# Gathering a block's last places for its first nodes alone, and a number of places of its own for each block

## The chip, the core and the metric

The kernel runs on one core of one Trainium2 chip. The metric is the device time of one execution, in microseconds. Before the change it is 5551.11 us, the median of three runs (5551.11 to 5564.75). One execution was recorded by the hardware profiler; its span, from the first to the last instruction, is 4044.6 us.

The core's engines run side by side, each through its own queue in order: TensorE (PE, with its weight loads PEld), VectorE (DVE), ScalarE (ACT), GpSimd (POOL) and SyncE (SP). Here SP issues plain DMAs, and POOL issues the indirect ones (row gathers by a list of indices).

## The reference

Sixteen graphs of 1024 nodes with 64 channels pass through four layers. Each layer normalizes the node features, and adds its result to them. The adjacency is sparse: each pair of nodes is joined with a chance of some 1.6%, and each node to itself. Layers 0, 1 and 3 are products with the weighted adjacency. Layer 2 is the one that matters here: a degree-dependent rule removes some neighbours, and each node then gets, channel by channel, a weighted sum of three quantiles over the neighbours that are left:

```python
sv = jnp.sort(jnp.where(valid[..., None], x[:, None, :, :], big), axis=2)
m = valid.sum(-1)
for tau, wt in zip((0.25, 0.5, 0.75), (0.25, 0.5, 0.25)):
    pos = jnp.clip(tau * (m - 1.0), 0.0)
    lo, hi, frac = floor(pos), ceil(pos), pos - floor(pos)
    agg += wt * (sv[lo] * (1 - frac) + sv[hi] * frac)
```

So for each node the features of its neighbours have to be brought together and sorted in part, for each of the 64 channels.

## The kernel before

Everything runs on one core, one graph after another, with up to four graphs in work at once. The function `direct_path` makes six streams, each a generator over the sixteen graphs:

- `adjacency` loads the adjacency by rows (SP), makes its transpose by PE and ACT, applies the removal rule, and stores for each node a row of 1024 keys (`keys_d`) that says which nodes are its neighbours. It also ranks the nodes by their number of neighbours, most first, and so makes `node`, the node at each rank, and `pos`, the rank of each node.
- `layers` computes layers 0 and 1 and the normalized input of layer 2, and stores the latter in memory (`h_d`, one row of 64 values per node, and a row 1024 of zeros).
- `neighbour_lists` takes the ranked nodes in eight blocks of 128, one node to a partition. For each block an indirect DMA loads the key rows (`k`, line 1019), and the DVE's MAX8 finds eight neighbours at a time (lines 1034 to 1050). The list becomes `index` (line 1056), where an unused place points to the row of zeros. The same stream makes the weights of the places (`far`, `wts`) and notes in `bad` whether a node has more neighbours than its block has places; if one has, another, general path computes everything anew after this one.
- `gathers` brings the rows: for each place of each block one indirect DMA on POOL writes 128 rows of 64 values, one to a partition, into `raw` (line 1165).
- `sorts` sorts, on the DVE, the places of `raw` against each other, with min and max between `raw` and a second buffer `other` (line 1208), and adds up the places that the quantiles need (line 1231). The pairs follow from the number of places (`cap`) of the group.
- `tail` gathers the results back into the order of the nodes (`res`, line 1251, eight indirect DMAs on POOL), and computes the rest of layer 2 and layer 3, with the transposed adjacency loaded again in tiles (`at`, by SP).

The blocks form five groups (line 38), each `(first block, blocks, places, fewest neighbours)`:

```python
GROUPS = [(0, 1, 38, 17), (1, 1, 20, 15), (2, 2, 18, 12), (4, 2, 16, 10), (6, 2, 13, 1)]
```

Blocks of a group share a `raw` tile and a sorting program. A graph has 38 + 20 + 2 x 18 + 2 x 16 + 2 x 13 = 152 row gathers. There is one `raw` buffer per group (`raws`, one buffer), so the gathers of group k of a graph can't be written before the sort of group k of the graph before has left it; they may run ahead of their own sort by about a graph.

The order of the instructions on each engine is written out when the program is built. A planner holds a clock per engine (`clk.dve`, `clk.pool`, ...), each stream says when it can go on, and the first stream in the list that is due gets the next turn. The planner counts 1.27 us for a row gather. What it fixes is the order alone: at run time each engine waits on semaphores for what its next instruction needs, and an instruction that waits holds up those behind it on its engine.

Of the kernel before, what the change touches and what calls it, by code (L numbers as in the profile page):

```python
# [7 lines left out]
F32 = mybir.dt.float32  # L8
F16 = mybir.dt.float16
BF = mybir.dt.bfloat16  # L10
I32 = mybir.dt.int32
# [6 lines left out]
P = 128  # L18
C = 64
# [19 lines left out]

E_ID, E_ONE, E_CAP, E_LOW, E_CN, E_Q, E_END = 0, 128, 256, 264, 272, 280, 320  # L40
J_ID, J_BIG, J_OFF, J_ST, J_ROW, J_ONE, J_PI, J_NI, J_END = 0, 128, 256, 384, 896, 1920, 2048, 2176, 2184
KB = 4


def _span(cap, low):

    return (low - 1) // 4, -(-3 * (cap - 1) // 4)
# [62 lines left out]
def _program(cap, low):  # L110


    home, out = [0] * cap, []
    for layer in _network(cap, low):
        for greater in (True, False):
            items = [(home[i], home[j], i, j) for i, j, a, b in layer if (a if greater else b)]
            out += [(greater, p) for p in _patterns(items)]
        for i, j, _, _ in layer:
            home[i] ^= 1
            home[j] ^= 1  # L120
    lo, hi = _span(cap, low)
    return out, _patterns([(home[q], 0, q, q - lo) for q in range(lo, hi + 1)])
# [587 lines left out]
def direct_path(ctx: ExitStack, tc: tile.TileContext, t: dict, out: bass.AP, flag):  # L710
# [3 lines left out]
    nc = tc.nc  # L714
# [3 lines left out]
    const = ctx.enter_context(tc.tile_pool(name="const", bufs=1))  # L718
    loads = ctx.enter_context(tc.tile_pool(name="loads", bufs=2))
    graph = ctx.enter_context(tc.tile_pool(name="graph", bufs=1))  # L720
    nodes = ctx.enter_context(tc.tile_pool(name="nodes", bufs=2))
# [4 lines left out]
    dram = ctx.enter_context(tc.tile_pool(name="dram", bufs=2, space=bass.MemoryType.DRAM))  # L726
# [57 lines left out]
    clk = Clock()  # L784

    def after(dve=0.0, pe=0.0, act=0.0, lat=0.3):

        clk.dve += dve
        at = clk.dve
        if pe:  # L790
            clk.pe = at = max(clk.pe, at) + pe
        if act:
            clk.act = at = max(clk.act, at) + act
        return at + lat
# [215 lines left out]
    def neighbour_lists(b):  # L1010


        g = state[b]
        ks = []

        def load_keys(i):
            if i < NB:
                k = lists.tile([P, N], F16, name="k", bufs=KB)
                nc.gpsimd.indirect_dma_start(k, None, g["keys_d"],  # L1019
                                             bass.IndirectOffsetOnAxis(ap=g["node"][:, i:i + 1], axis=0))  # L1020
                clk.pool = max(clk.pool, clk.dve) + 1.3
                ks.append((k, clk.pool + 3.5))

        for i in range(KB):
            load_keys(i)
        total = sum(n * -(-cap // 8) * 8 for _, n, cap, _ in GROUPS)
        found = lists.tile([P, total], F32, name="found", bufs=1)
        m = g["m"]
        o = 0
        for b0, n, cap, _ in GROUPS:  # L1030
            for i in range(b0, b0 + n):
                src, at = ks[i]
                yield at
                nc.vector.max(out=found[:, o:o + 8], in_=src)  # L1034
                clk.dve += 1.15
                yield clk.dve
                less, before = src.bitcast(I16), None
                for r in range(1, -(-cap // 8)):


                    least = found[:, o + 7:o + 8]
                    if r == 1:
                        ts(less, src, least, None, op0=ALU.subtract)  # L1043
                    else:
                        ts(less, less, before, least, op0=ALU.add, op1=ALU.subtract)  # L1045
                    before = least
                    most = nodes.tile([P, 8], U16, name="most")
                    nc.vector.max(out=most, in_=less.bitcast(U16))  # L1048
                    o += 8
                    ts(found[:, o:o + 8], most.bitcast(I16), 0.0, least, op0=ALU.min, op1=ALU.add)  # L1050
                    clk.dve += 1.8
                    yield clk.dve
                o += 8
                load_keys(i + KB)
        index = lists.tile([P, total], I32, name="index")
        ts(index, found, -1.0, float(N), op0=ALU.mult, op1=ALU.add)

        s = nodes.tile([P, 2, NB], F32, name="s")
        tt(s[:, 0], m, cap8, ALU.is_gt)
        tt(s[:, 1], m, low8, ALU.is_lt)  # L1060
        tt(s[:, 0], s[:, 0], s[:, 1], ALU.max)
        tt(bad, bad, s[:, 0], ALU.max)

        at = nodes.tile([P, 3, NB], F32, name="at")
        for k in range(3):
            ts(at[:, k], m, (k + 1) / 4, -(k + 1) / 4, op0=ALU.mult, op1=ALU.add)
        far = lists.tile([P, 3, QT], F32, name="far", bufs=1)
        o = 0
        for b0, n, cap, low in GROUPS:
            lo, hi = _span(cap, low)  # L1070
            k = hi + 1 - lo
            tt(far[:, :, o:o + k * n].rearrange("p t (q i) -> p t q i", i=n),
               cf[:, None, E_Q + lo:E_Q + hi + 1, None].to_broadcast([P, 3, k, n]),
               at[:, :, None, b0:b0 + n].to_broadcast([P, 3, k, n]), ALU.subtract)
            o += k * n
        act(far, far, AF.Abs)
        for k, w in enumerate((0.25, 0.5, 0.25)):
            act(far[:, k], far[:, k], AF.Relu, bias=wcol[:, k:k + 1], scale=-w)
        g.update(index=index)
        done.add(("index", b))  # L1080
        yield after(1.7, act=1.7)
        wts = lists.tile([P, QT], F32, name="wts", bufs=3)
        tt(wts, far[:, 0], far[:, 2], ALU.add)
        tt(wts, wts, far[:, 1], ALU.add)
        clk.dve += 0.4
        g.update(wts=wts)
        done.add(("lists", b))
# [65 lines left out]
    def gathers(b):  # L1153
        g = state[b]
        yield max(g["rows_at"], clk.pool)
        for k, (b0, n, cap, _) in enumerate(GROUPS):
            while not (b == 0 or ("sort", b - 1, k) in done):
                yield None
            raw = raws.tile([P, cap, n * C], F32, name=f"raw{k}")
            o = sum(c * -(-r // 8) * 8 for _, c, r, _ in GROUPS[:k])  # L1160
            clk.pool = max(clk.pool, clk.dve)
            for s in range(cap):
                for i in range(n):
                    at = o + i * -(-cap // 8) * 8 + s
                    nc.gpsimd.indirect_dma_start(raw[:, s, i * C:(i + 1) * C], None, h_ds[b % 3],  # L1165
                                                 bass.IndirectOffsetOnAxis(ap=g["index"][:, at:at + 1], axis=0))
                clk.pool += 1.27 * n
                if s % 4 == 3:
                    yield clk.pool - 3
            g[f"raw{k}"] = (raw, clk.pool + 4)  # L1170
            done.add(("gather", b, k))
        done.add(("gathers", b))
# [141 lines left out]
    wcol = const.tile([P, 3], F32, name="wcol")  # L1314
    for k, w in enumerate((0.25, 0.5, 0.25)):
        nc.vector.memset(wcol[:, k:k + 1], w)
    programs = [_program(cap, low) for _, _, cap, low in GROUPS]
    h_ds = [dram.tile([N + 1, C], F32, name=f"h_d{k}", bufs=1) for k in range(3)]
    for h_d in h_ds:
# [2 lines left out]
    def over_graphs(step, *needs):  # L1322
# [8 lines left out]
        over_graphs(layers, ("rows", 0), ("tail", 3)),  # L1331
        over_graphs(tail, ("sorts", 0)),
        over_graphs(gathers, ("index", 0), ("layers", 0)),
        over_graphs(neighbour_lists, ("keys", 0), ("gathers", 2), ("sorts", 3)),
        over_graphs(sorts, ("lists", 0)),
    ]
# [40 lines left out]
def _constants():  # L1377

    import numpy as np

    p = np.arange(P)
    ef = np.zeros((P, E_END), np.float32)
    ef[p, E_ID + p] = 1
    ef[:, E_ONE:E_ONE + P] = 1
    for b0, n, cap, low in GROUPS:
        ef[:, E_CAP + b0:E_CAP + b0 + n] = cap
        ef[:, E_LOW + b0:E_LOW + b0 + n] = low
    ef[:, E_CN:E_CN + NB] = 512 * N + N - 1 - (p[:, None] + P * np.arange(NB))
    ef[:, E_Q:E_END] = np.arange(E_END - E_Q)
    eh = np.zeros((P, J_END), np.float32)  # L1390
    eh[p, J_ID + p] = 1
    eh[p, J_BIG + p] = 2048
    eh[:, J_OFF:J_OFF + P] = 1
    eh[p, J_OFF + p] = 0
    eh[:, J_ST:J_ST + N // 2] = p[:, None] < np.arange(N // 2)
    eh[p, J_ST + p] = 2050
    eh[0, J_ROW:J_ROW + N] = -1024 - np.arange(N)
    eh[0, J_ONE:J_ONE + P] = 1
    eh[:, J_PI:J_PI + P] = p
    eh[:, J_NI:J_NI + NB] = p[:, None] + P * np.arange(NB)  # L1400
    return {**_general_constants(), "ef": ef, "eh": eh.astype(np.float16)}
# [73 lines left out]
```

## Time and profile before

| | |
|---|---|
| time, median of three runs | 5551.11 us |
| span of the profiled execution | 4044.6 us |
| DVE busy | 3476.7 us, 86% |
| POOL busy | 2951.5 us, 73% |
| PE busy | 2039.3 us, 50% |
| ACT busy | 1411.8 us, 35% |
| row gathers | 2432, 1096 ns each in the mean |
| key loads, result gathers on POOL | 128 and 128 |
| DMA | 372.57 MB, 92 GB/s in the mean |

Busy time is what an engine spent in recorded instructions. The gap between two instructions counts as idle time, and each group's row says what ended it: `<-issue` means that nothing was waited for that the profile shows, a name means that this instruction or DMA was awaited. A line of the waits reads: who waited, for what, how many us in total, how often, and the longest. The times in a timeline run from the start of the span. On POOL, the recorded length of an indirect DMA is POOL's own part of it.

### The profile page before, as it was taken

To read this page: it belongs to the slowest core of one execution; us is meant where nothing else is said; L and a number is where in the kernel's file an instruction comes from. 1 tells how busy PE (TensorE), PEld (TensorE's weight loads), DVE (VectorE), ACT (ScalarE), POOL (GpSimd) and SP (SyncE) were. 2 spreads that over 40 slices of the span, in tenths; PEclk is the share of its full clock that TensorE was granted. 3 is DMA by queue.
4 is the path that set the end of the run, shared out by engine and by line. 5 is a ranking of instruction groups with operands and counts; after the bars stand their busy time and mean duration, and the time that the engine had idled before them with its cause. 6 is when DMAs were issued, how large, how long until landed. Compare 5 with 4: busy or idle time off the path is not lost.

```text
span 4044.6 us, 34028 instructions
## 1 busy us (share of the span) xinstructions
PE 2039.3 (50%) x8387; PEld 980.5 (24%) x8387; DVE 3476.7 (86%) x9450; ACT 1411.8 (35%) x2594; POOL 2951.5 (73%) x2707
## 2 busy tenths in 40 slices
PE   7565574264735546473554647455454745540303
PEld 3223231121313122231322213132221313110101
DVE  2649998997999999998998989899998999997583
ACT  6544442342425333342533434253432424320000
POOL 0277777777777777777777777777777777777771
PEclk8676676576767767776675767677677776765656
DMA  2343543444434454543444444443535444442312
GB/s 88 115 87 88 120 111 53 110 92 90 117 55 126 86 120 94 109 104 50 125 90 115 94 96 114 53 138 74 130 83 105 108 62 112 76 109 37 68 26 53
DMA packets 251857, 372.57 MB, mean 92 GB/s; under 512 B 120160, under 2 KB 120352, under 8 KB 251648
## 3 DMA queue, kind: packets, MB, share of 16 engines
q0 software_dynamic: 92640, 117.88, 23.5%
q1 hardware_dynamic: 158864, 251.87, 18.4%
q8 instruction: 68, 1.11, 0.1%
q14 instruction: 141, 1.16, 0.1%
q10 hardware_dynamic: 144, 0.56, 0.0%
HBM read 256.84 MB, written 113.25 MB: 92 GB/s over the span
## 4 chain that ended last, share of the span: by engine, by line
POOL 41%; DVE 33%; issue 13%; PE 5%; DMA 5%; ACT 2%; DVEq 0%; POOLq 0%; ACTq 0%
POOL raw L1165 37%; DVE other L1208 8%; DVE raw L1208 7%; DVE most L1048 5%; PE pt L845 4%; POOL res L1251 3%; DMA raw<-h_d,index 2%; DVE found L1034 2%; DVE agg L1231 2%; DVE k L1045 1%; DMA k<-keys_d,node 1%; DVE found L1050 1%; DVE k L1043 1%; ACT adjt L1125 1%; DVE nb L874 1%
## 5 line engine op out<-in xcount | busy, mean ns | idle before, releaser
L1165 POOL DMA_INDIRECT raw<-h_d,index x2432 | 2666.0, 1096 | 757.5 <-issue 724.7
L1208 DVE TENSOR_TENSOR other<-raw 128x128 f32<-128x128 f32 (+7 forms) x1488 | 766.5, 533 | 73.4 <-DMA raw<-h_d,index 60.3
L1208 DVE TENSOR_TENSOR raw<-other 128x256 f32<-128x256 f32 (+10 forms) x1424 | 679.1, 490 | 4.3
L845 PE MATMUL pt<-adjt,ha 128*65 128x512 f32 (+1 forms) x1024 | 492.9, 644 | 299.3 <-DVE ha L1115 299.2
L881 PE MATMUL pt<-ef,a 128*128 128x128 f32 x1024 | 232.7, 391 | 389.4 <-ACT adjt L882 354.5
L1295 PE MATMUL tm<-at,ha 128*64 128x512 f32 x512 | 286.0, 677 | 54.9 <-DMA at<-adjt_d 52.4
L845 PEld LDWEIGHTS pt<-adjt,ha 128*65 128x65 f32 (+1 forms) x1024 | 150.0, 150 | 621.9 <-issue 569.6
L1048 DVE MAX8 most<-k 128x8 uint16<-128x1024 uint16 x224 | 275.0, 1228 | 7.7
L881 PEld LDWEIGHTS pt<-ef,a 128*128 128x128 f32 x1024 | 173.5, 203 | 441.8 <-ACT adjt L882 391.0
L922 PE MATMUL pt<-eh,nbt 128*128 128x512 f16 (+3 forms) x1024 | 210.0, 364 | 125.9 <-ACT nbt L911 125.4
L1019 POOL DMA_INDIRECT k<-keys_d,node x128 | 131.0, 1023 | 191.2 <-DVE node L1004 122.0
L956 ACT ACTIVATE nb<-pt 128x1024 f16<-128x1024 f32 x128 | 130.8, 1022 | 390.2 <-PE pt L952 248.3
L834 PE MATMUL pt<-ef,res 128*64 128x128 f32 x128 | 30.2, 418 | 425.7 <-DVE res L1255 335.3
L1034 DVE MAX8 found<-k 128x8 f32<-128x1024 f16 x128 | 156.3, 1221 | 99.2 <-DMA k<-keys_d,node 99.2
L887 ACT ACTIVATE nb<-nb 128x512 f16<-128x512 f16 x256 | 159.6, 628 | 206.2 <-DVE nb L876 119.4
L978 ACT ACTIVATE sink<-pt,neg 128x1024 f16<-128x1024 f32 x128 | 140.4, 1121 | 244.9 <-PE pt L973 244.9
L1208 DVE TENSOR_TENSOR other<-raw,other 128x256 f32<-128x256 f32 (+4 forms) x592 | 206.9, 354 | 5.4
L846 ACT COPY big<-pt 64x1024 f32<-64x1024 f32 (+1 forms) x32 | 32.2, 1007 | 505.9 <-PE pt L845 505.9
L1251 POOL DMA_INDIRECT res<-agg_d,pos x128 | 146.1, 1141 | 83.5 <-DMA agg_d<-agg 43.0
L927 ACT ACTIVATE ab<-pt,sf 128x512 f16<-128x512 f32 x256 | 161.8, 687 | 124.6 <-DVE gone L932 67.8
L1208 DVE TENSOR_TENSOR raw<-raw,other 128x256 f32<-128x256 f32 (+3 forms) x608 | 203.0, 338 | 0.0
L1208 DVE TENSOR_TENSOR raw<-other,raw 128x128 f32<-128x128 f32 (+5 forms) x560 | 196.1, 357 | 3.1
(154 smaller groups left out, 4068.0 us busy)
## 6 DMA issues: line engine op xcount, KB each, us to landing
a<-in_adj_dram SPq DMA_DIRECT2D x128, 512.0 KB, 3.6
adjt_d<-adjt SPq DMA_DIRECT2D x128, 512.0 KB, 5.7
at<-adjt_d SPq DMA_DIRECT2D x256, 256.0 KB, 3.8
raw<-h_d,index POOLq DMA_INDIRECT x2432
keys_d<-nb SPq DMA_DIRECT2D x128, 256.0 KB, 2.3
x<-in_x_dram SPq DMA_DIRECT2D x16, 256.0 KB, 2.9
h_d<-h SPq DMA_DIRECT2D x16, 256.0 KB, 4.2
agg_d<-agg SPq DMA_DIRECT2D x16, 256.0 KB, 2.8
```

The lines of the kernel that those rows point to most:

```text
L845: nc.tensor.matmul(p[p0:p0 + n, s], h[:, j, :n], adjt[:, j, s], start=j == 0, stop=j == NB - 1)
L881: nc.tensor.transpose(p[:, u * P:(u + 1) * P], a[:, j * P:(j + 1) * P], identf)
L887: act(nb[:, i, s], nb[:, i, s], AF.Copy, accum_out=mn[:, q, i:i + 1])
L922: nc.tensor.matmul(p[:, o:e], nbt[:, j, :], stair[:, :e - o], start=j % 4 == 0, stop=j % 4 == 3)
L927: act(ab[:, s], p[:, s], AF.Abs, bias=sf[:, 2 + q, i:i + 1], scale=2.0)
L978: act(sink, p, AF.Sign, bias=neg[:, i:i + 1], accum_out=over[:, i:i + 1])
L1034: nc.vector.max(out=found[:, o:o + 8], in_=src)
L1048: nc.vector.max(out=most, in_=less.bitcast(U16))
L1165: nc.gpsimd.indirect_dma_start(raw[:, s, i * C:(i + 1) * C], None, h_ds[b % 3], bass.IndirectOffsetOnAxis(ap=g["index"][:, at:at + 1], axi ...
L1208: tt(to, v0, v1, ALU.max if greater else ALU.min)
L1251: nc.gpsimd.indirect_dma_start(res[:, i, :], None, g["agg_d"], bass.IndirectOffsetOnAxis(ap=g["pos"][:, i:i + 1], axis=0))
L1295: nc.tensor.matmul(p[:C, :], ha[:, j, :C], ats[k], start=j == 0, stop=j == NB - 1)
```

## The change

Within a block the nodes stand in order of their number of neighbours, so a high place is used by the first few nodes alone. In block 0, with its 38 places, the first nodes decide the number. The change gives each block its own number of places, and brings the last 16 places of block 0 in another way:

- Blocks get 22, 20, 18, 17, 16, 14, 13 and 12 places. The places between this number and the group's `cap` are filled with zeros by ACT (`zcol`), as a gather of row 1024 would have done.
- For block 0, places 22 and 23 are brought for its first 64 nodes, 24 to 27 for the first 32, and 28 to 37 for the first 12: 2 x 64 = 128, 4 x 32 = 128 and 10 x 12 = 120 rows. Each of these sets is one indirect DMA, with one pair of node and place to a partition, into `packed`.
- For that, SP stores the three corners of `index` to memory (`pack_d`) and loads them back with one index to a partition (`pack`). And SP stores the packed rows to memory (`rows_d`, in the program after the ninth place is issued) and loads them into their places in `raw` (after the seventeenth).
- The table of places against which `bad` is judged (`E_CAP`) says the new numbers, node by node for block 0.

Row gathers of a graph go from 152 to 132, and 3 packed ones are added. The sorting programs and `GROUPS` stay as they are. The diff, without the table's part:

```diff
+PLACES = [22, 20, 18, 17, 16, 14, 13, 12]
+PACKS = [(22, 2, 64), (24, 4, 32), (28, 10, 12)]
...
         ts(index, found, -1.0, float(N), op0=ALU.mult, op1=ALU.add)
+        pack_d = dram.tile([len(PACKS), P], I32, name="pack_d")
+        pack = nodes.tile([P, len(PACKS)], I32, name="pack")
+        for l, (s0, ns, nn) in enumerate(PACKS):
+            nc.sync.dma_start(pack_d[l, :ns * nn].rearrange("(n s) -> n s", s=ns), index[:nn, s0:s0 + ns])
+        for l, (s0, ns, nn) in enumerate(PACKS):
+            nc.sync.dma_start(pack[:ns * nn, l:l + 1], pack_d[l, :ns * nn].rearrange("(n o) -> n o", o=1))
...
             clk.pool = max(clk.pool, clk.dve)
+            for i in range(n):
+                if PLACES[b0 + i] < cap:
+                    z = raw[:, PLACES[b0 + i]:cap, i * C:(i + 1) * C]
+                    nc.scalar.copy(z, zcol[:, :, None].to_broadcast([P, cap - PLACES[b0 + i], C]))
+                    clk.act = max(clk.act, clk.dve) + 0.2 + (cap - PLACES[b0 + i]) * C / 1400
+            if k == 0:
+                packed = nodes.tile([P, len(PACKS) * C], F32, name="packed", bufs=1)
+                for l, (s0, ns, nn) in enumerate(PACKS):
+                    nc.gpsimd.indirect_dma_start(packed[:ns * nn, l * C:(l + 1) * C], None, h_ds[b % 3],
+                                                 bass.IndirectOffsetOnAxis(ap=g["pack"][:ns * nn, l:l + 1], axis=0))
+                    clk.pool += 1.27
+                rows_d = dram.tile([len(PACKS), P, C], F32, name="rows_d")
             for s in range(cap):
+                if k == 0 and s == 9:
+                    for l, (s0, ns, nn) in enumerate(PACKS):
+                        nc.sync.dma_start(rows_d[l, :ns * nn], packed[:ns * nn, l * C:(l + 1) * C])
+                if k == 0 and s == 17:
+                    for l, (s0, ns, nn) in enumerate(PACKS):
+                        nc.sync.dma_start(raw[:nn, s0:s0 + ns, :],
+                                          rows_d[l, :ns * nn].rearrange("(n s) c -> n s c", s=ns))
                 for i in range(n):
+                    if s >= PLACES[b0 + i]:
+                        continue
+                    clk.pool += 1.27
                     at = o + i * -(-cap // 8) * 8 + s
                     nc.gpsimd.indirect_dma_start(raw[:, s, i * C:(i + 1) * C], None, h_ds[b % 3],
                                                  bass.IndirectOffsetOnAxis(ap=g["index"][:, at:at + 1], axis=0))
-                clk.pool += 1.27 * n
                 if s % 4 == 3:
                     yield clk.pool - 3
```

More of the change, by code (lines that the diff above doesn't have):

```diff
@@ L1078, in neighbour_lists @@
             act(far[:, k], far[:, k], AF.Relu, bias=wcol[:, k:k + 1], scale=-w)
-        g.update(index=index)
+        g.update(index=index, pack=pack)
         done.add(("index", b))
@@ L1316, in direct_path @@
         nc.vector.memset(wcol[:, k:k + 1], w)
+    zcol = const.tile([P, 1], F32, name="zcol")
+    nc.vector.memset(zcol, 0.0)
     programs = [_program(cap, low) for _, _, cap, low in GROUPS]
@@ L1385, in _constants @@
     for b0, n, cap, low in GROUPS:
-        ef[:, E_CAP + b0:E_CAP + b0 + n] = cap
+        ef[:, E_CAP + b0:E_CAP + b0 + n] = PLACES[b0:b0 + n]
         ef[:, E_LOW + b0:E_LOW + b0 + n] = low
+    for s0, ns, nn in PACKS:
+        ef[:nn, E_CAP] = s0 + ns
     ef[:, E_CN:E_CN + NB] = 512 * N + N - 1 - (p[:, None] + P * np.arange(NB))
```

## The prediction, made before the changed kernel ran

> **What bounds the kernel now.** I read the page's busy line first, then GpSimd's groups and timeline, then the DVE's waits by stretch.
>
> ```profile
> PE 2039.3 (50%) x8387; PEld 980.5 (24%) x8387; DVE 3476.7 (86%) x9450; ACT 1411.8 (35%) x2594; POOL 2951.5 (73%) x2707
> ...
> POOL 41%; DVE 33%; issue 13%; PE 5%; DMA 5%; ACT 2%; DVEq 0%; POOLq 0%; ACTq 0%
> ...
> L1165 POOL DMA_INDIRECT raw<-h_d,index x2432 | 2666.0, 1096 | 757.5 <-issue 724.7
> ```
>
> By busy share the DVE looks like the bound and POOL (GpSimd) looks slack. But the chain gives POOL more than the DVE, and almost all the idle time before POOL's gathers is "issue": nothing was waited for. The timeline shows what that is:
>
> ```profile
> 1999.92 0.95 POOL L1165 DMA_INDIRECT raw<-h_d,index  x1 [0.30 <-issue]
> 2001.18 1.01 POOL L1165 DMA_INDIRECT raw<-h_d,index  x1 [0.30 <-issue]
> 2002.49 0.97 POOL L1165 DMA_INDIRECT raw<-h_d,index  x1 [0.30 <-issue]
> ```
> ```profile
> 188.00:3955.00 3767.00, 2925.32 (x2672) 0.70 0.43 92
> ```
>
> Each gather pays 0.30 us between instructions. The last line is POOL from its first row gather to its last: 2672 instructions in 3767 us, 1.410 us each. Of the 842 us "idle" in it, 2672 x 0.30 = 802 is that gap. POOL is full from 188 to 3955. A graph has 152 row gathers, 8 key loads and 8 result gathers: 168 x 1.410 = 236.9 us. The DVE needs 3476.7 / 16 = 217.3. So POOL sets the period, and the DVE is close behind. Where the DVE waits, by stretch (columns: total us, times, longest; then busy and counts of PE, PEld, DVE, ACT, POOL):
>
> ```profile
> 0.00:240.00 240.00, 159.53 (x746) 81.02 (x746) 88.15 (x194) 132.52 (x247) 57.74 (x68) 0.79 0.34 92
> 240.00:3640.00 3400.00, 1801.99 (x7414) 863.50 (x7413) 3139.81 (x8519) 1265.91 (x2324) 2641.05 (x2406) 0.71 0.44 98
> 3640.00:4045.00 405.00, 77.75 (x229) 35.94 (x228) 248.76 (x739) 13.38 (x23) 252.75 (x235) 0.57 0.27 46
> ```
> ```profile
> DVE found L1034 <- DMA k<-keys_d,node: 96.0, 12, 15.9
> DVE wts L1083 <- ACT far L1078: 41.7, 9, 12.7
> DVE den L1131 <- PE pt L1120: 26.5, 13, 3.6
> DVE other L1208 <- DMA raw<-h_d,index: 10.0, 2, 9.5
> ...
> DVE res L1255 <- DMA res<-agg_d,pos: 6.0, 1, 6.0
> ```
> ```profile
> DVE other L1208 <- DMA raw<-h_d,index: 50.3, 6, 13.7
> DVE res L1255 <- DMA res<-agg_d,pos: 47.0, 2, 32.0
> ```
>
> The DVE is idle 152, 260 and 156 us in the three stretches, 568 together. The first list is the middle: 112 of its 260 end with something POOL issued (key loads 96, rows 10, results 6). The second is the end: 97 of 156.
>
> **The Trainium skill.** "DMA: Bandwidth & Descriptors", section "Anatomy of one DMA — SWDGE (gpsimd) path", gives a fixed cost of about 2.0 us per DMA, most of it the receipt of the write. This trace agrees for the queues on SP: 2.3 us to landing for keys_d, 4.2 for h_d. "Perfetto Trace Analysis", section "DMA Instruction — SWDGE (GPSIMD)", says that the recorded end is when the descriptors are written, not when data has moved. The trace fits: the gathers follow each other at 1.3 us without waiting for their own landings, so a removed gather saves POOL its whole pitch. "SBUF — State Buffer", section "SBUF: two separate sides", says a DVE instruction in a two-port mode keeps GpSimd from writing descriptors; the spread here (0.94 at least, 1.096 mean) would fit, but this trace does not show the cause, and I keep the mean.
>
> **The change, part by part.**
>
> *Removed gathers.* Places per block go from 38, 20, 18, 18, 16, 16, 13, 13 (152) to 22, 20, 18, 17, 16, 14, 13, 12 (132), and 3 packed gathers are added: 135, 17 fewer. 17 x 1.410 = 24.0 us of POOL per graph, 384 us in all. POOL's period becomes 151 x 1.410 = 212.9 us, under the DVE's 217.3. The bound changes hands, so the kernel can't gain the 384. What it can gain is the DVE's idle time that POOL causes.
>
> *The DVE's work.* The sorting programs still take caps of 38, 20, 18, 16, 13, so no DVE instruction of weight is removed or added: 3477 us stay.
>
> *Zero fills on ACT.* Four copies a graph: 1024 columns for block 0, then 64, 128 and 64. Nearest rows: 128x1024 copies take 1.01 to 1.05 us, tiny ones 0.17 to 0.30. About 1.8 us a graph, 29 in all, on an engine that is 35% busy. Each waits until the sort of the graph before has left the buffer. Behind it in ACT's queue stand copies that free PSUM for PE and the keys' activations; but the planner puts the fill where the DVE has already been told to finish that sort, so I take 0 to 2 us a graph and use 0.
>
> *Index packing on SP.* Three stores and three loads of a few hundred bytes, two landings in a row: 2 x 2.0 (the skill's price) to 2 x 4.2 (h_d), 4 to 8.4 us. For the last graph the index is written at 3575.5 us, while its gathers must start near 3953 - 160 x 1.41 = 3727: hidden by 150 us. Only in the first graph (index 188.2, first gather 188.7) is it bare: I take 6 us.
>
> *Rows through memory.* Three stores that wait for the packed gathers, three loads that wait for those stores. SP issues in order, so while it waits, the loads of the next adjacency rows, the stores of keys and the third layer's tiles queue behind it; PE and then the DVE would feel it. The packed gathers are issued ahead of nine others (nine x 1.41 = 12.7 us), and the loads come eight places (11 us) after the stores, against landings of 2 to 4.2 us. If POOL is where the planner thinks, SP waits for nothing. The planner counts 1.27 us for a gather that takes 1.41, so POOL may be late: 0 to 15 us a graph. Since POOL now has slack every graph in which to catch up, I take 1 us.
>
> *The sum*, by the DVE's idle time. Start: 13 fewer gathers before the first sort (38 to 25) give 13 x 1.25 = 16, less 6 for packing and the rest not waited for: -8. Middle: 112 at most; POOL still issues key loads among row gathers, so I leave a quarter of the 96 and charge 1 us a graph for SP: -112 + 24 + 14 = -74. The end: POOL's last 135 + 8 gathers take 143 x 1.41 = 202 us, less than the DVE's 249 busy us there, so the 50 us for rows go; of the results' 47 the last graph's 32 are mostly a chain with nothing beside it, 15 go: -65. Idle time 568 - 147 = 421, span 3477 + 421 = 3898 us, 147 less (3.6%).
>
> *From the span to the time.* The measured time is 5551.11 and the traced span 4044.6. No view shows the other 1506.5 us. If they lie outside the span, 147 us pass through unchanged: 5404. If untraced executions are longer throughout, the gain grows by 5551.11 / 4044.6 = 1.372 to 202: 5349. I take the middle, 5376, and keep both.
>
> **The rivals.**
>
> *More: untraced executions are longer because the gathers are.* 1506.5 us over 2703 POOL DMAs would be 0.56 each, 1.97 instead of 1.41. Then POOL stays far from the DVE, and the saving is 272 x 1.97 = 536: 5015. For it: POOL is the full engine. Against: nothing shows a gather of that length as usual.
>
> *Nothing to speak of.* The DVE's waits are replaced by others of its own (wts on ACT and den on PE are there already, 68 us in the middle), and only the end gains: 0 to 65 us, 5486 to 5551. For it: 86% busy leaves little. Against: 209 us of its idle time end with POOL's DMAs.
>
> *Slower: SP becomes the bound.* If each graph waits on SP for both chains (two pairs of landings, 8 to 16 us) and for a late POOL (15), less what overlaps, some 20 us x 16 = 320 are added against 147 saved: +173, 5724. For it: SP serves five streams in order, and both chains are new waits in it. Against: the slots left for the landings (12.7 and 11 us) exceed them, and a POOL with 4 us of slack a graph does not fall behind for long.
>
> **How the numbers follow.** Forecast 0.62, more 0.10, nothing 0.13 (half of it within 0.3%, half a small gain), slower 0.15. So faster 0.62 + 0.10 + 0.065, about 0.79; same 0.06; slower 0.15. The likeliest gives 5376. The range: upward it takes in the small gains, no change, and a first bit of the slower rival: 5570, with about one in eight above it. Downward, all 217 us (8 + 112 + 97) gone at 1.372 would be 298, so 5253; I go to 5215 for part of the "more" rival, with some 6 in 100 below.
>
> **What would show it.** In the new trace POOL's indirect DMAs should fall from 2688 to 2416, and its idle time should be ended in part by the DVE (sorts leaving their buffers), not only by issue. The DVE's share should rise from 86% to near 89%, the waits for k fall from 96 us to some 25, those for rows at the end from 50 to near none. ACT's fills should sum to about 29 us. Wrong would be: SP waiting for the packed gathers for more than a few us a graph, with new DVE waits on adjacency rows, on PE's third-layer sums or on keys; POOL still full; or a span that falls while the time does not.

## The result and the profile after

In the first comparison the changed kernel took 4721.66 us (median of 4 runs, 4694.21 to 4753.48) and the kernel before 5557.93 us (median of 4, 5551.11 to 5579.64): a ratio of 0.849, 95% interval 0.843 to 0.855. That is 836 us less, where 175 were forecast. The sign was right, the size was not, and the time lies below the range.

One plain fact is needed to read every number below. The kernel before took 5551 us only in that first comparison; in four later ones, which met other conditions, it took 4036 to 4040 us, and in one of them the changed kernel took 3933.35 us (median of 4, 3931.77 to 3937.70): a ratio of 0.976, interval 0.974 to 0.979. So there are two results to explain: 2.4% under the conditions that the profile of before shows, and 15% under the others. The later comparisons ran on four chips (numbers 0, 5, 4 and 9); the first one's is not on record, so it is open whether its conditions belong to one chip or to one time.

The page of the changed kernel from the first comparison, the lines that answer to those shown of before:

```profile
span 4717.7 us, 34351 instructions
...
PE 2141.2 (45%) x8387; PEld 1020.2 (22%) x8387; DVE 3494.2 (74%) x9451; ACT 1434.6 (30%) x2658; POOL 2620.3 (56%) x2435
...
DVE 48%; another core or an unknown queue 21%; issue 9%; PE 8%; POOL 6%; ACT 5%; DMA 3%; SPq 0%; DVEq 0%; ACTq 0%; POOLq 0%
...
L1197 POOL DMA_INDIRECT raw<-h_d,index x2112 | 2278.8, 1079 | 1236.9 <-issue 827.3
```

The span is 4717.7 us in an execution that took 4719.47: the time is all inside the span. The work is what was counted on: 2112 row gathers at 1079 ns, 48 packed ones, DVE at 3494 us as before. But the DVE is busy for 74%, not 89%, and POOL for 56%: nobody is full. And 21% of the chain's time goes to something that the profile cannot name.

The same kernel under the later conditions:

```profile
span 3929.9 us, 34351 instructions
...
PE 2016.5 (51%) x8387; PEld 961.6 (24%) x8387; DVE 3470.3 (88%) x9451; ACT 1434.4 (36%) x2658; POOL 2697.9 (69%) x2435
...
DVE 41%; POOL 14%; PE 7%; issue 5%; DMA 5%; ACT 2%; SPq 0%; DVEq 0%; ACTq 0%; POOLq 0%
...
L1197 POOL DMA_INDIRECT raw<-h_d,index x2112 | 2350.3, 1113 | 785.0 <-issue 754.6
```

Here the chain has gone over from POOL (41% before) to the DVE, and the DVE's share is 88%. The instructions are the same in both traces and last nearly as long (the DVE is busy 24 us more in the first, POOL 78 less; PE, at a mean clock of 0.657 against 0.706, 125 more, at 45% of the span). What makes up the 788 us is idle time: the DVE's is 1223.5 us against 459.6.

**Where the 788 us are.** Two lists of waits, first the changed kernel in the first comparison, then under the later conditions (columns: us in total, times, longest).

```profile
ACT big L850 <- remote: 447.3, 11, 77.8
...
ACT nb L960 <- remote: 328.9, 30, 34.1
...
PE pt L1130 <- ACT big L850: 209.9, 15, 32.7
DVE den L1141 <- PE pt L1130: 200.1, 14, 32.5
```
```profile
ACT big L850 <- PE pt L849: 464.3, 32, 18.3
...
DVE den L1141 <- PE pt L1130: 36.2, 15, 12.2
```

"remote" means that the wait ended with a semaphore update (the signal that work is done) near which no work was recorded to end. ACT's copy of the messages (L850) normally starts when PE's sums for them (L849) are done, and waits 18.3 us at most. In the first comparison it stood up to 77.8 us and pulled PE, then the DVE, behind it. One such place in the timeline of that comparison (start, duration, instruction, idle time before it):

```profile
2333.11 16.89 PE L849 MATMUL pt<-adjt,ha 128*65 128x512 f32 x32 [13.78 <-DVE ha L1125]
...
2372.05 0.95 POOL L1197 DMA_INDIRECT raw<-h_d,index  x1 [0.30 <-issue]
2373.30 0.95 POOL L1197 DMA_INDIRECT raw<-h_d,index  x1 [0.30 <-issue]
2380.24 1.01 ACT L850 COPY big<-pt 65x1024 f32<-65x1024 f32 x1 [48.69 <-remote]
...
2381.30 1.13 PE L1130 MATMUL pt<-ef,big 65*128 65x65 f32 x8 [31.31 <-ACT big L850]
...
2382.47 0.17 DVE L1141 TENSOR_SCALAR den<-pt 128x8 f32<-128x8 f32 x1 [32.39 <-PE pt L1130]
```

PE's 32 matmuls end at 2350.0. The semaphore update that tells ACT so stands in the trace at 2380.17, 30 us later, and ACT starts 0.07 us after it. Between the two, POOL issues gathers without a break (the last two are shown), to 2374.25. DVE then stands 32.39 us.

Over the whole trace I took, for each recorded semaphore update of an engine, the time since the last instruction of that engine that had ended:

```
                                 PE updates over 2 us late      DVE         ACT
before, as shown first           3 (all at the end)             3           3
changed, later conditions        3                              3           3
changed, first comparison        134, up to 45.2 us             23          3
```

Without the three at the end, PE's 131 fall into 70 moments, and the longest of each add up to 769 us. In 125 of the 131, POOL issued gathers between the end of the work and the update. That says less than it seems: stretches of the same lengths, laid at random over the same trace, have a gather in them in some 110 of 131. What stands out is POOL's next gather after the update. It is 7.1 us off in the middle case, against 1.2 us after those of PE's updates that came promptly and 0.9 us after a random moment. So many of the late updates get through when a burst of gathers is over. Not all do: after a third of them the next gather starts within 1.5 us.

Of the transfers this trace tells little, because records are missing from it. It has 13372 updates of GpSimd's transfers for 38896 packets that carry one (38836 in the later trace), and it lacks 17 to 24 of 100 updates of PE, DVE and ACT (PE has 1082, against 1308 later). So the next recorded update after a packet need not be its own, and no delay of a transfer can be read from it. Whether the missing records and the late updates have one cause, the recording itself included, was not tested.

The Trainium skill, "Perfetto Trace Analysis", section "Tensor Engine Instruction (MATMUL, LD_WEIGHTS)", says that the end of a matmul is estimated and that its semaphore update, and the time until all engines see it, lie outside the recorded window. So the trace alone can't say whether the matmuls ended late or their update travelled late. The DVE's late updates, whose ends are not modelled, speak for the update: 20 besides the three at the end, up to 6.8 us. ACT has none besides its three, so not every engine's updates were held. In the later traces end and update lie 0.01 us apart in 99 of 100 cases.

### The profile page after: what moved, and what is told of

Its sections match the earlier page's. It is cut to its first block, busy times and chain, and to the rows that moved or that the text cites. A ratio compares the mean times of both kernels' runs of the same rounds, so it can differ in the third digit from the quotient of the medians.

```text
span 4717.7 us, 34351 instructions
## 1 busy us (share of the span) xinstructions
PE 2141.2 (45%) x8387; PEld 1020.2 (22%) x8387; DVE 3494.2 (74%) x9451; ACT 1434.6 (30%) x2658; POOL 2620.3 (56%) x2435
## 4 chain that ended last, share of the span: by engine, by line
DVE 48%; another core or an unknown queue 21%; issue 9%; PE 8%; POOL 6%; ACT 5%; DMA 3%; SPq 0%; DVEq 0%; ACTq 0%; POOLq 0%
DVE other L1239 14%; DVE raw L1239 13%; POOL raw L1197 5%; DVE agg L1262 4%; DVE most L1052 3%; DVE found L1038 2%; PE pt L849 2%; DVE half L1262 1%; PE pt L855 1%; DVE nb L878 1%; ACT nb L891 1%; PE pt L1293 1%; PE tm L1326 1%; DVE k L1047 1%
## 5 line engine op out<-in xcount | busy, mean ns | idle before, releaser
L1197 POOL DMA_INDIRECT raw<-h_d,index x2112 | 2278.8, 1079 | 1236.9 <-issue 827.3
L849 PE MATMUL pt<-adjt,ha 128*65 128x512 f32 (+1 forms) x1024 | 494.7, 645 | 219.0 <-DVE ha L1125 91.4
L1326 PE MATMUL tm<-at,ha 128*64 128x512 f32 x512 | 305.0, 711 | 159.7 <-DMA at<-adjt_d 140.8
L885 PEld LDWEIGHTS pt<-ef,a 128*128 128x128 f32 x1024 | 185.8, 213 | 487.8 <-ACT adjt L886 393.1
L850 ACT COPY big<-pt 64x1024 f32<-64x1024 f32 (+1 forms) x32 | 32.2, 1007 | 777.5 <-remote 447.3
L849 PEld LDWEIGHTS pt<-adjt,ha 128*65 128x65 f32 (+1 forms) x1024 | 150.4, 150 | 545.5 <-issue 544.9
L838 PE MATMUL pt<-ef,res 128*64 128x128 f32 x128 | 30.5, 418 | 409.4 <-DVE other L1239 166.5
L886 ACT COPY adjt<-pt 128x512 f32<-128x512 f32 x256 | 137.7, 584 | 208.3 <-remote 108.9
```

The source lines that it names most:

```text
L849: nc.tensor.matmul(p[p0:p0 + n, s], h[:, j, :n], adjt[:, j, s], start=j == 0, stop=j == NB - 1)
L885: nc.tensor.transpose(p[:, u * P:(u + 1) * P], a[:, j * P:(j + 1) * P], identf)
L1326: nc.tensor.matmul(p[:C, :], ha[:, j, :C], ats[k], start=j == 0, stop=j == NB - 1)
```

## Experiments

Kernels compared together share the runs of before. All met the later conditions, so these runs test the mechanism that the forecast named. The expectations of places_only, pack_only and no_rows were written for 5551 us; their numbers do not apply, and they are judged by their kind. The forecast's theory: POOL's 168 transfers a graph set the period, 151 let the DVE set it. The rival: the gain comes from what else moves (order, waits, stores), or from each gather in proportion.

**The kernel before again.** `b_again` and, at the end, `before_three` are unchanged.

> The kernel before, unchanged, to see the profile of an execution like the timed ones. Theory A (the profile of before that was shown, span 4044.6 us, is not what the timed executions do): the span is 5551 us within 0.5%, and the 1500 us more are idle time of the DVE and of POOL, not longer instructions. Theory B (1500 us lie outside the traced span): the span is 4045 us again and the time 5551.

> The kernel before, unchanged, for its profile under whatever conditions this call meets. Theory A (the 5551 us of the first comparison belong to its conditions, which this call may or may not meet): the time equals the span plus about 2 us, 4037 or 5551; where it is 5551, semaphore updates of the other engines come after bursts of gathers in its trace, as in the changed kernel's. Theory B (the 1507 us lie outside the span): a span near 4040 beside a time near 5551.

Measured: 4042.13 us (ratio 1.0013, 1.000 to 1.003), span of the profiled run 4028.9; and 4035.81 us (0.9996, 0.998 to 1.001), span 4033.2 in an execution that took some 2 us more. Neither theory of `b_again` came out, because the 5551 us did not return. What follows: the time of a run is its span and some 2 us. That holds for every execution whose span is on record, the four of the changed kernel in the first comparison among them. It holds for the one on the page of before too: it took 4046.56 us itself, beside its span of 4044.6. So the 1506.5 us between 4044.6 and 5551.11 are the difference of two executions under two conditions, not time outside a span. (For the executions of 5551 to 5580 us no span is on record.)

**Each part alone.** `places_only` cuts blocks 2 to 7 to the places that the change gives them, without packing; `pack_only` packs block 0 and leaves the other blocks alone; `no_rows` is the changed kernel with places 22 to 37 of block 0 left at zero, without packed gathers and without their stores and loads, so it leaves out those rows.

```diff
 # places_only, against the changed kernel
-PLACES = [22, 20, 18, 17, 16, 14, 13, 12]
-PACKS = [(22, 2, 64), (24, 4, 32), (28, 10, 12)]
+PLACES = [38, 20, 18, 17, 16, 14, 13, 12]
+PACKS = []
...
 # pack_only, against the changed kernel
-PLACES = [22, 20, 18, 17, 16, 14, 13, 12]
+PLACES = [22, 20, 18, 18, 16, 16, 13, 13]
 # no_rows, against the changed kernel
-PACKS = [(22, 2, 64), (24, 4, 32), (28, 10, 12)]
+PACKS = []
...
```

> Only blocks 2 to 7 get fewer places (148 row gathers a graph for 152), block 0 keeps its 38, nothing is packed. Theory A, each gather left out is worth the same (836 us by 272 gathers is 3.07 us): 64 gathers fewer, 196 us less than before, about 5360 us. Theory B, the gain comes from block 0 alone, because its gathers are the ones waited for: within 60 us of before.

> Only block 0 is changed: 22 places and three packed gathers, the other blocks keep their places (139 row gathers a graph). Theory A, 3.07 us a gather: 208 fewer, 639 us less than before, about 4920 us. Theory B, the gain comes from block 0 alone: about 4720 us, as with the whole change.

> As changed, but the packed gathers and their twelve SP transfers a graph are left out, so places 22 to 37 of block 0 are zeros for all its nodes (132 gathers a graph; nodes with more neighbours lose them). Theory A, 3.07 us a gather: 48 gathers fewer than with the change, 4574 us, if the chains on SP cost nothing. If the chains cost 10 us a graph or more: under 4414 us.

Measured beside 4036.07: places_only 3967.32 (0.984, 0.981 to 0.987), pack_only 3950.89 (0.979, 0.977 to 0.981), no_rows 3973.18 (0.983, 0.981 to 0.985). Four gathers fewer a graph give 69 us; 13 fewer give 85; and 20 fewer with no store or load besides give 63. The gain does not go with the number removed, so the gathers are not each worth the same; nor does it come from block 0 alone, which places_only leaves as it was. What the stores and loads on SP cost can't be read from no_rows: it lacks them and is still some 40 us slower than the whole change. Its DVE is idle 503 us, against 460 in the changed kernel, and its POOL stood 166.5 us for ACT's L932 and 55.6 for the zero fills (L1174). Why its order came out so is open.

**The bound of each kernel.** `after_again` is the changed kernel; `after_cut` and `before_cut` leave out every odd weighted sum of a block after the third, 42 of 104 a graph, so the outputs are other numbers. That takes work from the DVE and none from POOL.

```diff
             for e, (s, i, j) in enumerate(places):
+                if e > 2 and e % 2:
+                    continue
```

> The changed kernel unchanged, on the same chip as three others. Where the kernel before takes about 4037 us: theory A (the forecast's mechanism: VectorE sets the period once GpSimd has 151 transfers a graph) says 3900 to 3950, a gain of 2 to 3.5%, about what either half of the change gave (3967 and 3951), since both halves already bring GpSimd under VectorE; theory B (the gathers are simply fewer, and each is worth the same, so the 85 us of 13 packed gathers a graph become more with 17) says 3880 or less. Where before takes about 5551 us: both say what was measured already, 4690 to 4750.

> The changed kernel without 42 of the 104 weighted sums of each graph (every odd one after the third of a block), so its outputs are other numbers. That takes 42 x 16 = 672 VectorE instructions of about 0.23 us, 155 us in all, 9.7 us a graph, from VectorE and nothing from GpSimd. Theory A (VectorE sets the period of the changed kernel): 100 to 150 us less than the changed kernel in the same call. Theory B (GpSimd or a chain of latencies still sets it): 0 to 30 us less, of which 10 are the last graph's.

> The kernel before without the same 42 weighted sums of each graph, so its outputs are other numbers: 155 us less for VectorE. Theory A (GpSimd sets the period of the kernel before, 236.9 us a graph against VectorE's 217.3): 0 to 25 us less than the kernel before, of which 10 are the last graph's. Theory B (VectorE sets it already): 100 to 150 us less.

Measured beside 4035.81: after_again 3933.35 (0.976, 0.974 to 0.979); after_cut 3844.68 (0.954, 0.952 to 0.956), 88.7 us less than after_again; before_cut 4026.41 (0.998, 0.997 to 0.999), 9.4 us less than before. The busy lines, first after_cut, then before_cut:

```profile
span 3826.5 us, 33654 instructions
...
PE 2024.4 (53%) x8387; PEld 980.9 (26%) x8387; DVE 3363.1 (88%) x8779; ACT 1428.6 (37%) x2658; POOL 2683.5 (70%) x2435
```
```profile
span 4031.3 us, 33405 instructions
...
PE 2017.1 (50%) x8387; PEld 968.9 (24%) x8387; DVE 3369.3 (84%) x8778; ACT 1412.2 (35%) x2594; POOL 2927.5 (73%) x2707
```

The same cut takes 107 us from the DVE in both (3470.3 to 3363.1; 3476.0 to 3369.3), not the 155 I had reckoned, so the 88.7 us lie below the 100 to 150 that theory A named. Sums in a row overlap: in the changed kernel they last 0.27 us each and start 0.20 us apart, and one removed saves 107 / 672 = 0.16 us of busy time. In the changed kernel the profiled span falls by 103 of these 107 and the DVE's idle time stays (459.6, then 463.4). In the kernel before, the span stays, and the DVE's idle time takes up the 107 (553, then 662). That settles who sets the period in each.

**How many gathers it takes.** `spare_17` and `spare_8` are the changed kernel with 17 or 8 gathers a graph more, whose rows go to a tile that nobody reads.

```diff
+                if k == 1 and s < 17:
+                    nc.gpsimd.indirect_dma_start(g["packed"][:, s % 3 * C:(s % 3 + 1) * C], None, h_ds[b % 3],
+                                                 bass.IndirectOffsetOnAxis(ap=g["index"][:, at:at + 1], axis=0))
+                    clk.pool += 1.27
```

> The changed kernel with 17 gathers a graph more, one after each of the first 17 of block 1, which fetch the same rows again into a tile that nobody reads: 168 GpSimd transfers a graph again, as before, with the changed kernel's VectorE work, stores and fills. Where the kernel before takes about 4037 us: theory A (the number of GpSimd transfers is what the change bought, 168 x 1.410 = 236.9 us a graph set the period again) says 4010 to 4050, the whole gain gone; theory B (the gain comes from something else that the change moves: other waits, other order) says 3930 to 3970. Where before takes about 5551 us: if the 836 us gained there are the 272 transfers at 3.07 us each, 5400 or more; if not, 4700 to 5100.

> The same with 8 spare gathers a graph, 159 transfers: 159 x 1.410 = 224.2 us a graph for GpSimd against 217.3 of VectorE work plus what VectorE waits. Where the kernel before takes about 4037 us: theory A (there is a knee: while GpSimd has slack a transfer more costs nothing) says 3930 to 3960; theory B (each transfer costs in proportion, (4036 - 3933) / 17 = 6.1 us of span for one more in each graph) says 3975 to 3990. Where before takes about 5551 us: if each transfer is worth 3.07 us, 4722 + 128 x 3.07 = about 5115.

Measured beside 4038.11: spare_17 4044.99 (1.002, 1.000 to 1.004), spare_8 3940.24 (0.978, 0.975 to 0.980). Each one's busy line and POOL by slices, 17 first:

```profile
PE 2018.5 (50%) x8387; PEld 976.7 (24%) x8387; DVE 3477.3 (86%) x9451; ACT 1435.8 (35%) x2658; POOL 2950.7 (73%) x2707
...
POOL 0177777777777777777777777777777777777771
```
```profile
PE 2030.4 (52%) x8387; PEld 974.1 (25%) x8387; DVE 3474.6 (88%) x9451; ACT 1433.5 (36%) x2658; POOL 2799.3 (71%) x2563
...
POOL 0177777777777777767777776777677776777760
```

A POOL that is full shows 7, not 9, for the 0.30 us between gathers. With 168 transfers it is 7 in every slice but the edges, and the whole gain is gone, with the changed kernel's packing, stores and fills all in place. With 159 some slices fall to 6, and the ratio is that of 151 within the intervals. So the time has a knee between 159 and 168 transfers. The periods say why: 159 x 1.410 = 224.2 us for POOL and 168 x 1.410 = 236.9, while the DVE with its waits takes some 234. That is a rough estimate, 217.3 us of work times 3285 / 3050, the changed kernel's middle stretch (shown below) over the DVE's work in it. places_only has 164 transfers, 231 us, and two thirds of the gain: near the knee the two periods are too close for this estimate to tell which is longer.

**Edits around it.** `cost_141` gives the planner the measured price, at both places that count a gather, and 11.3 us for the eight result gathers; `fill_pool` moves the zero fills to GpSimd.

```diff
 # cost_141
-                    clk.pool += 1.27
+                    clk.pool += 1.41
...
-        clk.pool = max(clk.pool, clk.dve) + 10.5
+        clk.pool = max(clk.pool, clk.dve) + 11.3
 # fill_pool
-                    nc.scalar.copy(z, zcol[:, :, None].to_broadcast([P, cap - PLACES[b0 + i], C]))
-                    clk.act = max(clk.act, clk.dve) + 0.2 + (cap - PLACES[b0 + i]) * C / 1400
+                    nc.gpsimd.memset(z, 0.0)
+                    clk.pool += 0.2 + (cap - PLACES[b0 + i]) * C / 1400
```

> The changed kernel with the planner's price of a gather at 1.41 us, as measured, in place of 1.27, and the eight result gathers at 11.3 in place of 10.5; the same instructions in another order. Theory A (the order is loose enough: what VectorE waits for is a few landings): within 15 us of the changed kernel. Theory B (at the low price the planner puts sorts ahead of landings that come later, and VectorE stands): 20 to 60 us less.

> The changed kernel with the four zero fills of each graph on GpSimd (memset) in place of ScalarE (copy). Theory A (GpSimd has slack, and the fills cost nothing where they are): within 15 us of the changed kernel. Theory B (GpSimd's gathers wait for a fill that stands in ScalarE's queue behind other work, and that reaches VectorE): 15 to 60 us less. Theory C (GpSimd's time counts after all): 20 us more or worse.

Measured: cost_141 3945.12 (0.979, 0.977 to 0.981), 12 us more than the changed kernel beside it; fill_pool 3931.31 (0.975, 0.973 to 0.977), which is the changed kernel's ratio within the intervals. cost_141's list of DVE waits is still worth a look:

```profile
DVE wts L1093 <- ACT far L1088: 106.2, 13, 12.9
...
DVE found L1038 <- DMA k<-keys_d,node: 3.3, 1, 3.3
```

The waits for key loads (80.9 us in the changed kernel) are gone, and waits for ACT have come in their place. A better price moved the idle time of the DVE; it removed none.

**Do many semaphore updates make them late?** `sem_load` adds two small stores after each row gather, on SP's queue.

```diff
+        load_d = dram.tile([2 * sum(PLACES), P, 1], F32, name="load_d")
+        sent = 0
...
+                    for u in range(2):
+                        nc.sync.dma_start(load_d[sent], zcol)
+                        sent += 1
```

> The changed kernel with two small stores more after each row gather, on SyncE's queue: 128 x 4 bytes of the zero column to a scratch array nobody reads, 264 a graph, 4224 in all, each with semaphore updates of its own. They leave VectorE, GpSimd and ScalarE their work and add semaphore updates by the thousand. Where the kernel before takes about 4037 us: theory A (the late semaphore updates of the first comparison come from their number: more of them make every engine's updates late here too) says 4100 us or more, with updates of other engines many us after the work that makes them; theory B (updates are taken at any rate that this kernel can make, and the lateness belonged to the conditions of that comparison) says 3930 to 3980 with updates as prompt as before. Where before takes about 5551 us: A says well over 4722, B about 4722.

Measured: 6655.86 us (ratio 1.645, 1.639 to 1.652). By its number that is theory A, but its trace shows another cause:

```profile
PE tm L1331 <- DMA at<-adjt_d: 1232.4, 128, 71.4
...
POOL res L1287 <- DMA agg_d<-agg: 1019.9, 16, 139.8
...
PE pt L885 <- DMA a<-in_adj_dram: 737.3, 32, 90.5
```

The engines wait for data: the loads and stores of SP's queue take their turn among 4224 stores. The semaphore updates stay prompt: PE, DVE and ACT each have the same three late ones, all at the end, and the trace holds some 38600 updates of GpSimd's transfers and 81500 of SP's. With those of PE, DVE and ACT that is over 19 a microsecond, where the kernels in the first comparison needed 11 to 13. So the number of updates alone does not make them late here. It raised SP's share only: GpSimd's updates came more slowly than in the first comparison (5.8 a microsecond, against 38896 / 4717.7 = 8.2). The experiment was a poor one in that it loaded the queue along with the semaphores.

## Why the prediction was wrong

**POOL sets the period of the kernel before: right.** before_cut and spare_17 show it from both sides.

**At 151 transfers the DVE sets it: right.** after_cut shows it, and spare_8 that the last eight removed were worth nothing measurable.

**The sum, under the conditions it was worked out for: right in kind, too large.** The DVE's idle time by the same three stretches (last one 405 us again), changed kernel, later conditions:

```profile
0.00:240.00 240.00, 155.37 (x755) 80.18 (x755) 97.30 (x202) 132.83 (x247) 55.15 (x63) 0.81 0.30 94
240.00:3525.00 3285.00, 1752.56 (x7323) 831.04 (x7322) 3050.05 (x8295) 1268.35 (x2349) 2426.11 (x2178) 0.71 0.38 97
3525.00:3930.00 405.00, 108.61 (x312) 50.40 (x310) 323.00 (x956) 33.23 (x62) 216.66 (x196) 0.59 0.26 64
```

Idle: 240 - 97.3 = 143, 3285 - 3050 = 235, 405 - 323 = 82. Against before that is -9, -25 and -74, where -8, -74 and -65 were forecast: -108 in place of -147. The end came out by its mechanism: the waits for rows there are gone, and 23.7 of the 47 us for results are left. The term that was mis-sized is the middle, and in it the key loads:

```profile
DVE found L1038 <- DMA k<-keys_d,node: 77.4, 12, 13.3
DVE den L1141 <- PE pt L1130: 22.8, 13, 2.7
DVE mid L1298 <- PE pt L855: 16.4, 1, 16.4
DVE node L1008 <- ACT m L1005: 15.7, 3, 10.2
DVE res L1286 <- DMA raw<-h_d,index: 13.2, 4, 4.1
DVE res L1286 <- DMA res<-agg_d,pos: 10.7, 3, 5.2
```

77.4 us are left of 96, where I kept a quarter. A POOL with slack does not bring the keys sooner: with slack or without, these waits sum to between 46 and 110 us over the whole span in all kernels of the later comparisons but one, and it is another order that brings them to 3.3 (cost_141). With those of `res` (13.2 and 10.7) the middle has 101 us of waits that end with POOL's DMAs; 112 stood there, and 24 were to be left. The largest wait that went is one that the forecast kept: the DVE's wait for ACT's `far`, 41.7 us before, is gone, while waits for PE's L855 (16.4) and ACT's m (15.7) came. So that POOL's fewer transfers shorten the time is shown (spare_17), but which waits would go was not foreseen.

**Zero fills and SP's chains: right in the main.** The fills sum to 28.9 us (29 forecast). SP waits 30.6 us in all for packed rows (1 us a graph was charged for SP, 1.9 were waited), and no long DVE wait ends with the rows that return. It also waits 49.0 us for the index to reach memory (`pack_d`); no DVE wait ends with that either. At the first graph POOL waits once for the packed index, 22.9 us where I took 6. That the start as a whole still gained the 8 us expected is luck: the first sort stood 25.9 us for its rows, and the waits for PE's sums into x (L851 before, L855 after) fell from 44.6 to 23.0, which the forecast did not have. The rival that had SP as the bound has no line for it.

**The price of a landing.** The 2.0 us is stated, where the prediction took it from, for DMAs that GpSimd issues. It was used for SP's, where this case shows 2.3 us for one tensor and 4.2 for another; the 4 to 8.4 us for two landings cover both.

**From the span to the time: here it failed.** The step read: "If they lie outside the span, 147 us pass through unchanged: 5404. If untraced executions are longer throughout, the gain grows by 5551.11 / 4044.6 = 1.372". Both were wrong. The changed kernel's time lies in its span, and what lengthens that is not the instructions: the gathers take 1079 ns in the mean there, against 1096 in the profile of before. It is waits that the profile of before has not got at all. Under those conditions the excess over the later ones is 5557.93 - 4035.81 = 1522 us for the kernel before and 4721.66 - 3933.35 = 788 for the changed one. So of the 836 us gained, by this subtraction, 102 are the forecast mechanism and 734 are a smaller excess. The rival "More" had the direction and the wrong ground: it wanted longer gathers.

**What is shown and what is argued.** Shown: the conditions differ; in the first, recorded updates of PE come up to 45 us after the modelled end of its work; these moments add up to 769 us, near the excess of 788, though not all of them need be on the path. Argued only: that bursts of gathers hold the updates back, and that the kernel before loses more because its gathers hardly pause. Its POOL stops for over 2 us 11 times in its profile, the changed kernel's 29 times later and 66 times in the first comparison, so late updates would find fewer openings. There is no trace of the kernel before under the first conditions to check it on, and they did not come back in any later comparison. What makes them is open.

## What to carry to other kernels

A profile stands for a measured time only if its span is that time to within a few microseconds. If it is not, the profile is of another condition, and neither adding the difference nor scaling by it turns a saving in the one into a saving in the other; the range must then hold both. To learn which engine sets the period, take work from the other and see whether the time stays; to learn what a removed instruction is worth, put some back as dead work and look for the knee. Instructions taken from a full engine pay only down to the next engine's period, here within the first nine of 17.

## What the runs showed of the hardware

- PE's semaphore updates can stand in the trace tens of microseconds after the modelled end of its work (131 in one execution, up to 45.2 us), and the DVE's up to 6.8 us, while the DVE's busy time is the same within 1% (3494.2 and 3470.3 us). The sign is waits put down to "remote" (447.3 us for one copy), with no engine full. The cause is open.
- Row gathers of 128 rows of 256 bytes follow each other at 1.41 us, 0.30 us of it between instructions, so a full POOL showed as 73% busy over the span (spare_17).
- 4224 stores of 128 x 4 bytes on SP's queue lengthened the kernel by 2722 us (6655.86 against 3933.35 in another comparison), 0.64 us each; PE's wait for the tiles `at` grew from 41.4 to 1232.4 us.
- Weighted sums in a row on the DVE are worth 0.16 us of busy time each when removed, though one lasts 273 ns in the mean.
